# Layer 0's convolutions: the values' 1x1 products ahead of the first depthwise product, and VectorE's taps dealt anew

## The chip, the cores and the metric

The kernel runs on one core of a Trainium2 chip. The metric is the device time of one execution in microseconds, as the median of several runs. The kernel has 82,178 instructions on five engines that run side by side, each through its own list in order: TensorE (PE, with its weight loads as PEld), VectorE (DVE), ScalarE (ACT), GpSimd (POOL) and SyncE (SP), which issues DMAs.[...]

## The reference

Four layers are applied one after the other to `x` of shape 2 x 128 x 64 x 64, each as `x = x + layer(groupnorm(x))`. Only layer 0 is touched:

```python
xn = biasfree_ln(x, ln1_w)
qkv = conv1x1(xn, w_qkv)                      # 128 -> 5 * 128 channels
qkv = conv_general_dilated(qkv, w_dw, 3x3, 'SAME', feature_group_count=5 * c)
q1, k1, v, q2, k2 = jnp.split(qkv, 5, axis=1)
q1, q2, k1, k2 = map(l2norm_tokens, (q1, q2, k1, k2))
attn1 = softmax(q1 . k1 * temperature)        # over the 4096 positions, 4 heads of 32 channels
attn2 = softmax(q2^T . k2 * temperature)      # over channels
out = attn1 . v  +  v . attn2
out = conv1x1(biasfree_ln(conv1x1(out, w_po), ln2_w), w_proj) + b_proj
```

So five groups of 128 channels (q1, k1, v, q2, k2) each go through a 1x1 product over channels, and then through nine taps of a 3x3 convolution with weights of their own for each channel.

## The kernel before, in words

Channels lie on the 128 partitions, the 4096 positions (64 rows of 64) along the free dimension. A sample's feature map is handled in two halves of 32 rows. For sample 0 and then for sample 1 the function `_layer0` runs `convolutions`, then `attention` (the softmax over positions, by far the longest part), then `finish` (the output products, layer norm and the addition to x). The finish of sample 0 is held back and runs inside the convolutions of sample 1.

`pointwise(pad, grp, half)` makes one *frame*: the 1x1 products of one group and one half, written into a padded image of 34 rows by 66 columns. GpSimd zeroes the borders (three memsets, L1582 to L1585), TensorE makes the products (L1591, ten instructions) and ScalarE copies them from PSUM into the frame in four pieces (L1598).

The 3x3 convolution of a half is done in one of two ways. `depthwise` does it on TensorE: 144 small matmuls with diagonal weights (L1613; the trace shows 288 instructions, since each float32 product is two), accumulating into two pairs of PSUM banks. `taps` does it on VectorE: a multiplication for the first tap (L1648) and eight multiply-adds (L1650), each over 128 x 2048 elements. It is a generator, and each `next` issues one tap. Three of the ten halves go to VectorE: the first half of k1 and both halves of the values v, 27 taps a sample. The other seven go to TensorE in the order `[(1,1), (0,0), (0,1), (3,0), (4,0), (3,1), (4,1)]` of (group, half); I number these stages n = 0 to 6.

PSUM is used in three pairs of banks (`sp()`, in turn) and two single banks (`acc(0)`, `acc(1)`). A depthwise product takes two pairs; a frame takes one pair and both single banks, `acc(0)` twice. After a depthwise product for q1 or k1 (n = 0, 1, 2), `in_place` copies the result out, eight 32 x 512 copies on ScalarE from the first pair and eight on VectorE from the second (L1633). After one for q2 or k2 (n = 3 to 6), ScalarE copies the first pair and VectorE the second (`copy`, L1624).

In stage n the program issues, in this order: the depthwise product; the copies out of it, and the frame for stage n + 2; ScalarE's sums of squares (L1638); what belongs to this stage alone; and then some of VectorE's taps. To this stage alone belong: a value frame and six steps of the earlier sample's finish at n = 0, the rest of the finish at n = 1, the other value frame and the norms of q1 and k1 (L1757 to L1760) at n = 2, the scaling of q1 (L1764) at n = 3, the token products of q2 and k2 (`products`, L1678 and L1688) at n = 4 and 6, and the transposes of the values (`value_tiles`, L1662) at n = 5 and 6. The order on each engine is that of the program (`_in_order`, L1328), so a copy waits behind the taps issued before it. How many taps each stage issues is the tuple at the end of the loop, one for sample 0 and one for sample 1.

Frames for TensorE lie in two buffers of the tag "pad", those for VectorE in two buffers of the tag "vpad"; each frame is 8,976 bytes a partition. The tile `qk2` (16,384 bytes) holds a half of q2 and k2 from n = 3 on.

Of the kernel before, what the change touches and what calls it, by code (L numbers as in the profile page):

```python
# [10 lines left out]
F32 = mybir.dt.float32  # L11
# [5 lines left out]
B, C, H, W = 2, 128, 64, 64  # L17
S = H * W
CH = 512
# [1429 lines left out]
def _layer0(ctx, tc, X, a, cst, worst, there, dram):  # L1449
# [8 lines left out]
    def sp():  # L1458
        n = at["pair"]
        at["pair"] = (n + 1) % 3  # L1460
        return banks[:, 2 * n : 2 * n + 2, :]

    def acc(n):
        return banks[:, 6 + n, :]
# [31 lines left out]
    v = one.tile([128, S], F32, name="v")  # L1496
# [3 lines left out]
    def inverse_norm(ss, name):  # L1500
        n = small.tile([128, 1], F32, tag=name, name=name)
        nc.vector.tensor_reduce(n, ss, AX.X, ALU.add)
        _power(nc, small, n, n, 1e-24, 0.0, mhalf)
        return n
# [72 lines left out]
    def frame(pool, tag="pad", bufs=2):  # L1577
        return pool.tile([128, H // 2 + 2, W + 2], F32, tag=tag, name=tag, bufs=bufs)

    def pointwise(pad, grp, half):  # L1580

        nc.gpsimd.memset(pad[:, :, 0:1], 0.0)  # L1582
        nc.gpsimd.memset(pad[:, :, W + 1 : W + 2], 0.0)
        edge = 0 if half == 0 else H // 2 + 1
        nc.gpsimd.memset(pad[:, edge, :], 0.0)  # L1585
        first, to = (0, 1) if half == 0 else (H // 2 - 1, 0)
        for r0, n in ((4 * ROWS, 1), (0, ROWS), (ROWS, 2 * ROWS), (3 * ROWS, ROWS)):
            ps = sp() if n > ROWS else acc(int(r0 == 0)).rearrange("p (o c) -> p o c", o=1)
            for i in range(0, n, ROWS):
                rows = min(ROWS, n - i)  # L1590
                nc.tensor.matmul(  # L1591
                    ps[:, i // ROWS, : rows * W],
                    w_qkv[:, grp * C : (grp + 1) * C],
                    xn[:, (first + r0 + i) * W : (first + r0 + i + rows) * W],
                    start=True,
                    stop=True,
                )
            nc.scalar.copy(  # L1598
                pad[:, to + r0 : to + r0 + n, 1 : W + 1],
                ps.rearrange("p k (h w) -> p (k h) w", w=W)[:, :n, :],  # L1600
            )
            yield

    def depthwise(grp, pad):


        ps = [sp() for _ in range(2)]
        for t in range(9):
            for c in range(4):
                for r in range(4):  # L1610
                    rows, to = slice(32 * r, 32 * r + 32), slice(32 * c, 32 * c + 32)
                    y0 = c * ROWS + t // 3
                    nc.tensor.matmul(  # L1613
                        ps[r // 2][to, r % 2, :].rearrange("p (h w) -> p h w", w=W),
                        diag[rows, grp, t, :],
                        pad[rows, y0 : y0 + ROWS, t % 3 : t % 3 + W],
                        start=(t == 0),
                        stop=(t == 8),
                    )
        return ps  # L1620

    def copy(out, in_):
        turn[0] += 1
        (nc.scalar.copy if turn[0] % 2 else nc.vector.tensor_copy)(out, in_)  # L1624

    def in_place(ps, half, out, p):


        for i in range(4):
            for n, engine in enumerate((nc.scalar.copy, nc.vector.tensor_copy)):  # L1630
                r, c = 2 * n + p, (i + 2 * n) % 4
                cols = slice((4 * half + c) * CH, (4 * half + c + 1) * CH)
                engine(out[32 * r : 32 * r + 32, cols], ps[n][32 * c : 32 * c + 32, p, :])  # L1633

    def squares(pool, t, at):
        junk = pool.tile([128, 2 * CH], F32, tag="junk", name="junk", bufs=1)
        n = t.free_size()
        nc.scalar.activation(junk[:, :n], t, AF.Square, accum_out=at)  # L1638

    def taps(grp, half, to, pad):  # L1640

        cols = slice(half * S // 2, (half + 1) * S // 2)
        out = to[:, cols].rearrange("p (h w) -> p h w", w=W)
        for t in range(9):
            x = pad[:, t // 3 : t // 3 + H // 2, t % 3 : t % 3 + W]
            tap = wd[:, 9 * grp + t : 9 * grp + t + 1]
            if t == 0:
                nc.vector.tensor_scalar_mul(out, x, tap)  # L1648
            else:
                nc.vector.scalar_tensor_tensor(out, x, tap, out, ALU.mult, ALU.add)  # L1650
            yield

    def squares_of(pool, out, half, at):
        for i in range(2 * half, 2 * half + 2):
            squares(pool, out[:, i * 2 * CH : (i + 1) * 2 * CH], at[:, i : i + 1])
# [41 lines left out]
    def convolutions(pool, b, before):  # L1697


        ss = small.tile([128, 2, 4], F32, tag="ss", name="ss")  # L1700
        ss2 = small.tile([128, 2, 4, 2], F32, tag="ss2", name="ss2")
        gram = None
        order = [(1, 1), (0, 0), (0, 1), (3, 0), (4, 0), (3, 1), (4, 1)]
        kpad = frame(pool, "vpad")
        run(pointwise(kpad, 1, 0))
        first = taps(1, 0, k1, kpad)
        frames = [frame(pool) for _ in range(2)]
        run(pointwise(frames[0], *order[0]))
        next(first)
        run(pointwise(frames[1], *order[1]))  # L1710
        by_vector = first

        def values_of(half):
            pad = frame(pool, "vpad")
            run(pointwise(pad, 2, half))
            return taps(2, half, v, pad)

        qk = None
        for n, (grp, half) in enumerate(order):
            ps = depthwise(grp, frames.pop(0))  # L1720
            following = iter(())
            if n + 2 < len(order):
                frames.append(frame(pool))
                following = pointwise(frames[-1], *order[n + 2])
            if grp >= 3:
                if grp == 3:
                    qk = pool.tile([128, 2, 4, CH], F32, tag="qk2", name="qk2", bufs=1)
                for p in range(2):
                    copy(qk[:, grp - 3, 2 * p : 2 * p + 2, :], ps[p])
                run(following)  # L1730
                for r in range(4):
                    squares(pool, qk[:, grp - 3, r, :], ss2[:, grp - 3, r, half : half + 1])
            else:
                out = (q1, k1)[grp]
                in_place(ps, half, out, 0)
                next(following, None)
                in_place(ps, half, out, 1)
                run(following)
                squares_of(pool, out, half, ss[:, grp, :])
            if n == 0:  # L1740
                by_vector = chain(by_vector, values_of(0))
                for _ in range(FIRST_PART):
                    next(before, None)
            elif n == 1:
                run(before)
            if n == 4:
                gram = acc(1)
                run(products(pool, qk, 0, gram))
            elif n == 5:
                run(value_tiles(0))  # L1750
            elif n == 6:
                run(value_tiles(1))
                run(products(pool, qk, 1, gram))
            if n == 2:
                squares_of(pool, k1, 0, ss[:, 1, :])
                by_vector = chain(by_vector, values_of(1))
                nq = inverse_norm(ss[:, 0, :], "nq1")  # L1757
                nk = inverse_norm(ss[:, 1, :], "nk1")
                sc = small.tile([128, 1], F32, tag="sc", name="sc")
                nc.vector.scalar_tensor_tensor(sc, nq, nk, temp, ALU.mult, ALU.mult)  # L1760
            if n == 3:
                for c in range(0, NCH, 2):
                    cols = slice(c * CH, (c + 2) * CH)
                    nc.vector.tensor_scalar_mul(q1[:, cols], q1[:, cols], sc)  # L1764
            for _ in range(((5, 5, 5, 4, 4, 4, 0), (2, 6, 6, 4, 4, 4, 0))[b > 0][n]):
                next(by_vector, None)

        own = small.tile([128, 4, C], F32, tag="own", name="own", bufs=1)
        nc.vector.tensor_mul(
            own,  # L1770
            gram.rearrange("p (r c) -> p r c", r=4),
            blocks.unsqueeze(1).to_broadcast([128, 4, C]),
        )
        return ss2, own
# [206 lines left out]
    def run(gen):  # L1981
        for _ in gen:
            pass

    def chain(*gens):
        for g in gens:
            yield from g
# [3 lines left out]
    with _in_order(tc):  # L1991
        first = normalize(0)
# [585 lines left out]
```

## Time and profile before

| | us |
|---|---|
| median of 3 runs | 4053.4 (4051.79 to 4055.28) |
| the profiled execution | 4055.8 |
| its span, first to last instruction | 4054.0 |
| normalizing sample 0 | 0 to 33.6 |
| convolutions of sample 0 | 33.6 to 193 |
| attention of sample 0 | 193 to 780 |
| convolutions of sample 1, with the finish of sample 0 | 780 to 975 |
| attention of sample 1 | 975 to 1568 |
| layers 1 to 3 | 1568 to 4054 |

A row of the profile in order of time reads: start, duration, engine, line, operation, output <- inputs, partitions x elements, how many such instructions in a row; and in brackets how long the engine had been idle before it and what ended that. A table of stretches has for each stretch its length, then the busy time of each engine with its number of instructions, then TensorE's granted clock as a share of full speed, the busy share of the DMA engines, and GB/s.

### The profile page before, as it was taken

The numbers are of one execution on the slowest core, as the hardware profiler recorded it, in microseconds if no ns is written. First come the engines' busy times: TensorE is split into PE (matmuls) and PEld (weight loads), VectorE is DVE, ScalarE is ACT, GpSimd is POOL, SyncE is SP. The second block draws the span as 40 slices with busy tenths as digits, with TensorE's granted clock in tenths as the row PEclk, the third lists the DMA queues.
The fourth block names the chain that finished last, engine by engine and source line by source line (L and its number), as shares of the span: only waits on it lengthen the run. The fifth ranks groups of instructions, "written<-read, shape, count | busy, mean of one in ns | idle before, by whom it ended". The sixth has DMA issues, their size and how long they took to land.

```text
span 4054.0 us, 82178 instructions
## 1 busy us (share of the span) xinstructions
PE 3872.8 (96%) x35214; PEld 1324.0 (33%) x35214; DVE 3198.9 (79%) x3572; ACT 3242.3 (80%) x3955; POOL 90.7 (2%) x145
## 2 busy tenths in 40 slices
PE   7899999989999998997998999999999999999998
PEld 4511221244121114445665222232222322222222
DVE  5699999766999998996766787777777777776666
ACT  4489889735899993325654899999999999999998
POOL 1000000010010001000000000000000000000000
PEclk9999999999999998998998999999999999999999
DMA  1199960000000000003663110110002000110000
GB/s 50 17 197 187 185 105 2 1 2 2 2 2 2 2 2 13 6 1 150 278 259 112 53 40 27 45 55 27 27 29 73 25 27 30 39 52 6 6 6 4
DMA packets 193128, 217.59 MB, mean 54 GB/s; under 512 B 30441, under 2 KB 154345, under 8 KB 188658
## 3 DMA queue, kind: packets, MB, share of 16 engines
q1 hardware_dynamic: 192754, 212.25, 20.3%
q8 instruction: 278, 4.55, 0.5%
q14 instruction: 96, 0.79, 0.1%
HBM read 178.64 MB, written 98.57 MB: 68 GB/s over the span
## 4 chain that ended last, share of the span: by engine, by line
PE 65%; DVE 7%; ACT 2%; issue 2%; POOL 0%; SPq 0%; DMA 0%; ACTq 0%; POOLq 0%; DVEq 0%
PE ps_acc L2293 25%; PE ps_s L2270 18%; PE ps L1842 5%; PE ps L1850 5%; PE ps_bank L710 2%; DVE sums L1873 2%; PE ps_z L1008 2%; DVE e L950 2%; PE ps_t L640 1%; PE ps_bank L590 1%; PE ps_bank L681 1%; PE ps_bank L1062 1%; PE ps_acc L2151 1%; PE ps_acc L2197 1%; PE ps_pe L925 1%
## 5 line engine op out<-in xcount | busy, mean ns | idle before, releaser
L2284 ACT ACTIVATE weights<-ps_s 128x1024 f32<-128x1024 f32 x1920 | 1781.4, 1062 | 75.6 <-PE ps_s L2270 75.5
L2293 PE MATMUL ps_acc<-weights,vt 128*32 128x512 f32 x8192 | 1092.7, 605 | 0.0
L1873 DVE TENSOR_TENSOR sums<-sums,weights 128x2048 f32<-128x2048 f32 x384 | 855.3, 2287 | 15.8 <-ACT weights L1921 14.5
L2270 PE MATMUL ps_s<-q,k 64*128 64x512 f32 x4096 | 831.0, 470 | 3.7 <-DMA k<-stack 2.5
L1921 ACT ACTIVATE weights<-ps 128x1536 f32<-128x1536 f32 x512 | 740.6, 1446 | 8.9 <-PE ps L1850 8.9
L2270 PEld LDWEIGHTS ps_s<-q,k 64*128 64x128 f32 x4096 | 348.4, 184 | 935.7 <-ACT weights L2284 809.2
L1850 PE MATMUL ps<-q,k 32*64 32x512 f32 x8192 | 577.0, 615 | 21.6 <-ACT weights L1918 19.4
L1842 PE MATMUL ps<-weights,vt 128*32 128x512 f32 x4096 | 548.3, 607 | 0.0
L2242 DVE SCALAR_TENSOR_TENSOR exp_z<-exp_z,exp_m 128x1024 f32<-128x1024 f32 x384 | 469.1, 1222 | 9.3
L1918 ACT ACTIVATE weights<-ps 128x512 f32<-128x512 f32 x512 | 306.8, 599 | 107.1 <-DVE sums L1873 38.6
L2226 DVE TENSOR_SCALAR exp_i<-ps_s 128x1024 int32<-128x1024 f32 x128 | 156.8, 1225 | 216.2 <-PE ps_s L2270 216.0
L1850 PEld LDWEIGHTS ps<-q,k 32*64 32x64 f32 x8192 | 120.8, 130 | 456.4 <-ACT weights L1918 403.4
L2293 PEld LDWEIGHTS ps_acc<-weights,vt 128*32 128x32 f32 x8192 | 161.9, 108 | 309.3 <-issue 308.5
L1842 PEld LDWEIGHTS ps<-weights,vt 128*32 128x32 f32 x4096 | 84.4, 108 | 392.7 <-issue 379.4
L662 DVE SCALAR_TENSOR_TENSOR X<-g,w,X 128x2048 f32<-128x2048 f32 x84 | 197.4, 2351 | 2.6
L1873 DVE TENSOR_TENSOR sums<-weights 128x2048 f32<-128x2048 f32 x64 | 145.9, 2289 | 39.8 <-ACT weights L1921 39.3
L2246 DVE SCALAR_TENSOR_TENSOR weights<-exp_z,exp_i 128x1024 f32<-128x1024 f32 x128 | 156.8, 1225 | 15.9 <-ACT weights L2284 0.5
L2242 DVE SCALAR_TENSOR_TENSOR exp_z<-exp_m 128x1024 f32<-128x1024 f32 x128 | 156.0, 1219 | 0.0
L1008 PE MATMUL ps_z<-w_ri,e 128*32 128x128 f32 x2048 | 137.3, 408 | 14.1 <-DVE e L950 11.9
L1613 PE MATMUL ps<-pad,diag 32*32 32x512 f32 x4032 | 142.3, 604 | 4.1 <-ACT vt L1624 3.7
L1591 PE MATMUL ps<-xn,w_qkv 128*128 128x512 f32 (+1 forms) x200 | 87.3, 583 | 22.5 <-ACT pad L1598 14.1
L950 DVE TENSOR_SCALAR e<-ps_pe 32x136 f32<-32x136 f32 (+1 forms) x352 | 104.3, 296 | 4.9
(304 smaller groups left out, 2976.7 us busy)
## 6 DMA issues: line engine op xcount, KB each, us to landing
w_ri<-w_r SPq DMA_DIRECT2D x16, 2112.0 KB, 8.0
w_ri<-w_i SPq DMA_DIRECT2D x16, 2112.0 KB, 13.6
stack<-qs SPq DMA_DIRECT2D x64, 256.0 KB, 2.1
q<-stack SPq DMA_DIRECT2D x128, 128.0 KB, 2.5
k<-stack SPq DMA_DIRECT2D x128, 128.0 KB, 2.6
stack<-ks SPq DMA_DIRECT2D x32, 256.0 KB, 2.2
w_r<-in_L_conv_kr_w SPq DMA_DIRECT2D x15, 528.0 KB, 12.6
w_r<-in_L_conv_kr_x SPq DMA_DIRECT2D x15, 528.0 KB, 12.6
```

Source lines behind the costliest of these rows:

```text
L662: nc.vector.scalar_tensor_tensor(xi, g[:, i : i + H // 2, j : j + W], w8[:, s : s + 1], xi, ALU.mult, ALU.add)
L950: nc.vector.tensor_scalar_mul(out, got[of, :, s], sign)
L1008: nc.tensor.matmul(out.rearrange("p (n f o) -> p n f o", n=2, f=2), e[:, s, 2 * j : 2 * j + 2, :].rearrange("p f x -> p (f x)"), w.rearran ...
L1842: nc.tensor.matmul(out[rows, :], lhs(rows), w[:, j, :], start=first, stop=stop)
L1850: nc.tensor.matmul(bank[64 * h : 64 * h + 64, :], k1[rows, kt * 128 + 64 * h : kt * 128 + 64 * h + 64], q1[rows, qb * CH : (qb + 1) * CH], ...
L1873: nc.vector.tensor_add(parts[p].rearrange("p j c -> p (j c)"), t.rearrange("p j c -> p (j c)"), w.rearrange("p j c -> p (j c)"),)
L1918: nc.scalar.activation(held[n][:, 0, :], single, AF.Exp)
L1921: nc.scalar.activation(held[n][:, 1:, :], three, AF.Exp)
L2242: nc.vector.scalar_tensor_tensor(z, x, n, m, ALU.add, ALU.mult)
L2270: nc.tensor.matmul(ps[j // 2][:, j % 2, :], g.k[kt // 4][rows, j // 2, keys], g.q[qb][rows, j // 2, :], start=True, stop=True,)
L2284: nc.scalar.activation(w[0], ps[p], AF.Exp)
L2293: nc.tensor.matmul(g.ac[32 * j : 32 * j + 32, :], g.vt[:, kt, j // 2, i : i + 2, :].rearrange("p a d -> p (a d)"), w[:, i, :], start=(at = ...
```

## The change

The first half of k1 gets its frame from the tag `qk2`, which is free until stage 3, so that both buffers of "vpad" can hold the two value frames at once. All five first frames are then made before the loop: k1's, those of stages 0 and 1, and the two value frames. Behind each of the last four, VectorE is given two taps of k1, so eight of the nine are issued before the first depthwise product. The value frames disappear from stages 0 and 2. Nineteen taps are left for the loop, dealt in new numbers: 3, 3, 3, 2, 4, 4 in sample 0 (before 5, 5, 5, 4, 4, 4, of which the last call is empty) and 0, 2, 4, 4, 4, 5 in sample 1 (before 2, 6, 6, 4, 4, 4).

```diff
         order = [(1, 1), (0, 0), (0, 1), (3, 0), (4, 0), (3, 1), (4, 1)]
-        kpad = frame(pool, "vpad")
+        kpad = pool.tile([128, 8 * CH], F32, tag="qk2", name="kpad", bufs=1)
+        kpad = kpad[:, : (H // 2 + 2) * (W + 2)].rearrange("p (h w) -> p h w", w=W + 2)
         run(pointwise(kpad, 1, 0))
         first = taps(1, 0, k1, kpad)
         frames = [frame(pool) for _ in range(2)]
-        run(pointwise(frames[0], *order[0]))
-        next(first)
-        run(pointwise(frames[1], *order[1]))
-        by_vector = first
+        by_vector = [first]
+
+        def ahead():
+            for _ in range(2):
+                next(first)
 
         def values_of(half):
             pad = frame(pool, "vpad")
             run(pointwise(pad, 2, half))
-            return taps(2, half, v, pad)
+            by_vector.append(taps(2, half, v, pad))
+
+        for n in range(2):
+            run(pointwise(frames[n], *order[n]))
+            ahead()
+        for n in range(2):
+            values_of(n)
+            ahead()
+        by_vector = chain(*by_vector)
...
             if n == 0:
-                by_vector = chain(by_vector, values_of(0))
                 for _ in range(FIRST_PART):
                     next(before, None)
...
             if n == 2:
                 squares_of(pool, k1, 0, ss[:, 1, :])
-                by_vector = chain(by_vector, values_of(1))
                 nq = inverse_norm(ss[:, 0, :], "nq1")
...
-            for _ in range(((5, 5, 5, 4, 4, 4, 0), (2, 6, 6, 4, 4, 4, 0))[b > 0][n]):
+            for _ in range(((3, 3, 3, 2, 4, 4, 0), (0, 2, 4, 4, 4, 5, 0))[b > 0][n]):
                 next(by_vector, None)
```

## The prediction

> **What bounds the kernel now.** I read the busy shares first, then the stretches of the kernel, and then the instructions in order of time in the only two stretches that the diff touches: the convolutions of sample 0 (33.6 to 193 us) and of sample 1 (780 to 975 us). First the page's shares, then the stretch table (busy us of PE, PEld, DVE, ACT, POOL; clock; DMA):
>
> ```profile
> PE 3872.8 (96%) x35214; PEld 1324.0 (33%) x35214; DVE 3198.9 (79%) x3572; ACT 3242.3 (80%) x3955; POOL 90.7 (2%) x145
> ...
> 33.60:193.00 159.40, 144.50 (x2305) 84.64 (x2311) 95.46 (x83) 69.10 (x127) 6.30 (x25) 0.95 0.01 2
> 780.00:975.00 195.00, 165.68 (x2494) 101.08 (x2492) 117.62 (x167) 73.71 (x134) 12.79 (x40) 0.96 0.01 2
> ```
>
> DMA is idle there (0.01), and VectorE and ScalarE are 38 to 60% busy, so neither is the bound by sum. TensorE is busy 91% and 85%, so the stretch ends when its in-order list ends, and what counts are its waits. Sample 0 in order of time:
>
> ```profile
> 48.65 3.92 PE L1591 MATMUL ps<-xn,w_qkv 128*128 128x64 f32 x10 [0.73 <-ACT pad L1598]
> ...
> 62.37 5.62 DVE L1633 COPY k<-ps 32x512 f32<-32x512 f32 x8 [17.11 <-PE ps L1613]
> ...
> 69.28 6.55 PE L1591 MATMUL ps<-xn,w_qkv 128*128 128x64 f32 x9 [3.17 <-ACT pad L1598]
> ...
> 90.97 10.48 PE L1613 MATMUL ps<-pad,diag 32*32 32x512 f32 x286 [0.18 <-ACT q L1633]
> ...
> 114.22 9.75 PE L1613 MATMUL ps<-pad,diag 32*32 32x512 f32 x288
> ...
> 126.12 1.23 DVE L1624 COPY qk<-ps 128x1024 f32<-128x1024 f32 x1
> ...
> 127.76 9.77 PE L1613 MATMUL ps<-pad,diag 32*32 32x512 f32 x288
> ```
>
> A frame's 1x1 products take 3.92 us of TensorE, 4.65 from one frame to the next at the start (44.00, 48.65). VectorE idles 17.11 us there. The value frame's products inside the loop (69.28) are dearer: they wait 3.17 us for a copy queued on ScalarE and then run 6.55 instead of 3.92 us. Sample 1 has the same places, worse:
>
> ```profile
> 816.83 0.89 DVE L1511 BATCH_NORM_STATS2 ln_st<-ps 128x6 f32<-128x128 f32 x4 [7.04 <-PE ps L1962]
> ...
> 891.87 2.08 PE L1591 MATMUL ps<-xn,w_qkv 128*128 128x512 f32 x2 [6.08 <-ACT vpad L1598]
> ...
> 893.87 11.67 PE L1613 MATMUL ps<-pad,diag 32*32 32x512 f32 x288
> ...
> 906.15 1.23 DVE L1624 COPY qk<-ps 128x1024 f32<-128x1024 f32 x1
> ```
>
> **What the Trainium skill says.** "TensorE: Matmul & The Clock Gate", Architectural detail: ScalarE and VectorE are strict FIFO. The trace agrees: the copy of 126.12 starts when the last tap before it ends (126.09), 2.2 us after its depthwise product. The same page, What's actually happening: after an idle window of about 3.4 us the array runs at half clock until it has been busy about as long. The trace agrees in part: after 3.17 us idle the granted clock was 0.52 (69.2 to 75.8), 0.71 (108.4 to 114.2) or 1.00 (811 to 815). "VectorE: DVE Perf Modes", tier table: single-source fp32 runs at twice the rate of two-source. Here the first tap takes 1.28 us, the others 2.35 (2.38 from one to the next).
>
> **The change, part by part.** I call En the end of depthwise product n, read as the start of the TensorE group behind it: before, sample 0 has E0 62.19, E1 85.89, E2 101.38, E3 123.90, E4 137.46; sample 1 has 803.99, 843.64, 875.63, 905.47, 919.01.
>
> *Start.* Two more frames before depthwise 0: 2 x 4.65 = +9.3 us. Their ScalarE copies (2.3 us a frame) are inside that pace; no DMA moves, so SP has nothing of it. E0 becomes 71.5 and 813.3. Eight taps of the first keys, 1.3 + 7 x 2.38 = 18 us, run from 43.98 (785.85 in sample 1) to 62 (804): wholly in VectorE's idle time, cost nothing; without that cover each would cost up to 2.38. The memsets of two more frames (POOL, 0.16 us each) come early; the key frame's new place in qk2 has to be free only by depthwise 3, long after its ninth tap.
>
> *Sample 0, n=0.* Without the value products the stage is like n=1 before, which had none: E2-E1 = 15.49 us (1x1 products 3.9 us, then the wait until ScalarE and VectorE have emptied both PSUM pairs, 5.8 us after En, then 9.65 us). Before, E0 to E1 took 23.70: -8.2. VectorE: eight copies 5.62 and three taps (6.1) fit into 15.5. E1 = 87.0, E2 = 102.5, so +1.1 so far.
>
> *Sample 0, n=2.* The value products go here too. The norms keep their chain (ScalarE's squares, GpSimd's powers): the taps start at E2+12.82 (114.20). Three taps, 7.13: E2+19.95, but depthwise 3 now ends at E2+15.49. The VectorE copy of qk is behind those taps, 4.5 us late, done at E2+21.2. Depthwise 4 needs the PSUM pair it frees (its own products would let it start at E2+19.35). So 1.9 us of new wait, and E4 = E2 + 21.25 + 9.65 = E2+30.9 against 36.08 before: -5.2. Together E4 133.4 against 137.46: **-4.1 us**.
>
> *Sample 1, n=0.* Behind the pointwise products stands finish of sample 0. VectorE's first bn_stats waits until 816.83, 12.84 after E0, for products queued behind the value frame. Now TensorE reaches those at E0+3.8, VectorE is free at E0+5.8: start at 819.15, +2.3 instead of +9.3. The finish then has its own pace (3.8 us a chunk, VectorE, GpSimd, TensorE in turn) and E0 to E2 is otherwise unchanged: E2 = 877.9. Taps moved out of n=0 cost nothing (VectorE waited 1.45 us before E1); two instead of six at n=1 take away VectorE's 5.4 us delay at E2 (881.03 against 875.63).
>
> *Sample 1, n=2.* Four taps: E2+12.82+9.51 = E2+22.3, copy done E2+23.6, depthwise 4 ends at E2+33.3 = 911.2 against 919.01: **-7.8 us**. The new TensorE wait before depthwise 4 is 4.3 us, which can put the clock to half: depthwise 3 of before (893.87), after such waits, took 11.67 instead of 9.76, 1.9 more. Bounds 0 and 3; I take 1.3.
>
> *Behind it.* The copy after E4 comes 2.6 us late in sample 1 (four taps at n=3), done at E4+3.8; the product that needs its bank runs from E4+4.3: hidden. E4 to E5 is 26.04 in both samples and ends on ScalarE's squares and the token copies, which don't change. The fifth tap at n=5 in sample 1 ends 0.7 us after E6, so the second value transposes start late; ScalarE reads them only behind 4 us of squares: hidden, 0 to 0.7. The attention's first weights tile now lies on qk2: its exponential may wait 1 us, where the next one has 4.6 us of idle: hidden. Later stages only shift.
>
> Sum: -4.1 - 7.8 + 1.3 = **-10.6 us**. The profiled execution took 4055.8 (span 4054.0), 2.4 above the median of 4053.4; so 4045.2 for it, and **4042.8** as a median. The 18.6 us paid in front are the sure part; 8.2, 5.2, 7.0 and 10.1 less 1.3 have to be earned back in four stages.
>
> **Rivals.**
> (a) A part isn't earned. If the finish in sample 1 starts no earlier (its PSUM bank or GpSimd pacing it), 7 us are lost: 4049.8. For it: its VectorE-GpSimd chain has idle gaps everywhere. Against: the 7.04 us wait names TensorE. Within 0.2%.
> (b) VectorE's late copies don't hold depthwise 4, because the tail of the taps hides elsewhere; then all of E3 counts, -5.9 and -12.1: -18, 4035.4. Against: strict order on VectorE, and two PSUM pairs of three are taken by depthwise products.
> (c) Slower: the clock. Depthwise 1 to 4 of both samples now start after waits of 1 to 4 us without value products between. From about 2.5 us lost on each of the eight (20 us) the change is slower than before by 8; the row at 893.87 shows 1.9, and at 69.2 to 75.8 a whole group ran at 0.52. At 3 us each: 4053.4 - 11.9 + 24 = 4065.5. Against: depthwise 2 (90.97) followed such a wait at clock 1.00.
> (d) It doesn't do what it says: hardly, the order is fixed per engine by the program.
>
> **How the numbers follow.** Likeliest case 0.66 (4038 to 4047, of it 0.08 above 4045.3), (b) 0.08, (a) 0.13, (c) 0.11, (d) 0.02. A measurement of this kernel can tell 0.2%, 8.1 us, from no change: below 4045.3 is faster, above 4061.5 slower. Faster 0.66, same 0.08 + 0.13 + 0.02 = 0.23, slower 0.11. The range goes from 4036 to 4053: it takes in (a) and the clock's bound, and leaves out most of (b) and (c), under 0.2.
>
> **What would show it.** Right: four 1x1 groups of 4.65 us and eight key taps ahead of depthwise 0, E0 near 71.5 and 813; E0 to E1 15.5 us in sample 0; first bn_stats of the finish near 815 (819 less sample 0's gain); VectorE's qk copy behind n=2's taps, and TensorE waiting for it before depthwise 4, 2 and 4 us. E6 4 us earlier in sample 0, 10 to 12 in sample 1. Wrong: TensorE at half clock through whole depthwise products; a wait of the first frames for the attention's tiles in sample 1; attention stretches (587 and 593 us) of another length.

## The result, and the profile after

| | median, us | runs | ratio to before, 95% |
|---|---|---|---|
| before | 4052.6 (4046.74 to 4055.28) | 6 | |
| after | 4036.61 (4032.69 to 4038.05) | 6 | 0.9962 [0.9949, 0.9975] |
| after, once more | 4038.11 (4034.54 to 4042.41) | 6 | 0.9968 [0.9956, 0.998] |

The change makes the kernel faster, by 16 us in the first comparison and by 12.7 in the second (there against 4050.82, the median of 37 runs of before). Forecast were 4042.8 for the median, with a range of 4036 to 4053, and 10.6 us for the gain; so the first median lies 0.6 us above the range's lower end. The profiled execution of after took 4035.3 us, its span is 4033.5.

The page of after, busy shares of the engines:

```profile
PE 3863.0 (96%) x35214; PEld 1317.6 (33%) x35214; DVE 3198.8 (79%) x3572; ACT 3242.7 (80%) x3955; POOL 90.5 (2%) x145
```

Every count is the same as before (35,214, 3572, 3955, 145): the change only moves work. So the gain must lie in the waiting or in TensorE's clock. To see it, both kernels have to be cut at the same events. I cut each convolution stretch from the first tap on the first half of k1 (L1648) to VectorE's product that makes `own` (L1769 before, L1777 after), the last of `convolutions`. Before, in the table of stretches (length, then busy PE, PEld, DVE, ACT, POOL; clock; DMA):

```profile
43.98:192.65 148.67, 135.26 (x2280) 79.62 (x2288) 91.93 (x71) 64.25 (x119) 3.65 (x23) 0.94 0.01 2
785.85:972.55 186.70, 158.72 (x2456) 98.90 (x2464) 113.17 (x159) 69.63 (x127) 11.77 (x31) 0.95 0.01 2
```

After, the same cuts:

```profile
39.44:183.93 144.49, 134.71 (x2280) 78.85 (x2288) 92.02 (x70) 64.65 (x119) 3.01 (x17) 0.98 0.01 2
773.69:954.03 180.34, 159.71 (x2456) 99.25 (x2464) 113.08 (x159) 70.02 (x127) 11.06 (x25) 0.97 0.01 2
```

The two stretches together shrink from 335.37 to 324.83 us, by 10.5. TensorE's busy time in them is 293.98 before and 294.42 after, so its idle time fell from 41.4 to 30.4. (The split is rough: the same work counts as longer busy where the clock is low, and the clock column is lower before; and rows such as the one at 72.04 below, 10.48 us for 286 instructions where 288 take 9.76 elsewhere, hold some waiting.) VectorE has 205.1 us of work in both. The forecast's 10.6 us are in these two stretches; what the first comparison shows beyond them is dealt with below.

Sample 0 of after in order of time, the lines that answer to those shown of before:

```profile
40.76 16.68 DVE L1650 SCALAR_TENSOR_TENSOR k<-kpad,wd,k 128x2048 f32<-128x2048 f32 x7
...
53.43 3.92 PE L1591 MATMUL ps<-xn,w_qkv 128*128 128x64 f32 x10 [0.73 <-ACT vpad L1598]
57.29 9.76 PE L1613 MATMUL ps<-pad,diag 32*32 32x512 f32 x288
...
67.15 5.62 DVE L1633 COPY k<-ps 32x512 f32<-32x512 f32 x8 [9.71 <-PE ps L1613]
...
72.04 10.48 PE L1613 MATMUL ps<-pad,diag 32*32 32x512 f32 x286 [0.17 <-ACT k L1633]
...
110.68 7.12 DVE L1650 SCALAR_TENSOR_TENSOR v<-vpad,wd,v 128x2048 f32<-128x2048 f32 x3
...
117.83 1.22 DVE L1624 COPY qk<-ps 128x1024 f32<-128x1024 f32 x1
119.11 9.72 PE L1613 MATMUL ps<-pad,diag 32*32 32x512 f32 x284 [0.92 <-DVE qk L1624]
```

The keys' taps (40.76) now run while TensorE makes the four frames; VectorE still idles 9.71 us before its first copy, where it idled 17.11. Depthwise 1 (72.04) follows depthwise 0 with only the normal wait for PSUM: the value products with their 3.17 us wait and their 6.55 us are gone from this place. The last two lines are the new wait: the copy of qk stands behind three taps, and depthwise 4 cannot go on until that copy has emptied its PSUM pair. (Four of its 288 instructions, 1.05 us, run before the row's wait of 0.92 us; counted from the end of the 1x1 products the delay is 1.9 us.)

In sample 1 of before, the copies behind stage 1 came late, because five taps stood before them (E2 was at 875.63):

```profile
869.10 11.90 DVE L1650 SCALAR_TENSOR_TENSOR k<-vpad,wd,k 128x2048 f32<-128x2048 f32 x5
881.03 5.62 DVE L1633 COPY q<-ps 32x512 f32<-32x512 f32 x8
```

Sample 1 of after in order of time:

```profile
806.97 0.89 DVE L1511 BATCH_NORM_STATS2 ln_st<-ps 128x6 f32<-128x128 f32 x4
...
866.14 5.62 DVE L1633 COPY q<-ps 32x512 f32<-32x512 f32 x8 [5.56 <-PE ps L1613]
...
878.77 9.51 DVE L1650 SCALAR_TENSOR_TENSOR v<-vpad,wd,v 128x2048 f32<-128x2048 f32 x4
...
888.31 1.22 DVE L1624 COPY qk<-ps 128x1024 f32<-128x1024 f32 x1
...
889.59 10.99 PE L1613 MATMUL ps<-pad,diag 32*32 32x512 f32 x284 [3.23 <-DVE qk L1624]
```

The finish's first bn_stats starts without a wait, 5.8 us after E0 (801.15); before it waited 7.04 us for TensorE and came 12.84 us after E0. The copies at 866.14 now wait for TensorE; before they came 5.4 us after TensorE was done. The last lines are the new wait in its larger form: four taps, the copy of qk, then TensorE released after 3.23 us (4.2 us after the end of the 1x1 products) and running 10.99 us for 284 instructions (9.72 in sample 0).

**Where the profiled difference of 20.5 us lies.** The stages of the two first profiles, cut at the same events (us):

| | before | after | difference |
|---|---|---|---|
| start to k1's first tap | 43.98 | 39.44 | -4.5 |
| convolutions of sample 0 | 148.67 | 144.49 | -4.2 |
| attention of sample 0 | 593.20 | 589.76 | -3.4 |
| convolutions of sample 1 | 186.70 | 180.34 | -6.4 |
| attention of sample 1 | 565.68 | 565.40 | -0.3 |
| its finish | 46.66 | 45.53 | -1.1 |
| layer 1 | 258.11 | 256.03 | -2.1 |
| layers 2 and 3 | 2211.0 | 2212.5 | +1.5 |

Attention ends here at its last copy of q, the finish of sample 1 at the first product of layer 1 (L590 in before), layer 1 at the first `ps_py` product of layer 2 (L883). Half of the difference lies in stages that the diff does not touch. Whether that is a consequence or chance was the first question.

### The profile page after: what moved, and what is told of

The parts are those of the page before. It is cut to its first block, busy times and chain, and to the rows that moved or that the text cites. A ratio compares the mean times of both kernels' runs of the same rounds, so it can differ in the third digit from the quotient of the medians.

```text
span 4033.5 us, 82173 instructions
## 1 busy us (share of the span) xinstructions
PE 3863.0 (96%) x35214; PEld 1317.6 (33%) x35214; DVE 3198.8 (79%) x3572; ACT 3242.7 (80%) x3955; POOL 90.5 (2%) x145
## 3 DMA queue, kind: packets, MB, share of 16 engines
q8 instruction: 278, 4.55, 0.5%
## 4 chain that ended last, share of the span: by engine, by line
PE 77%; DVE 10%; ACT 4%; issue 4%; POOL 0%; SPq 0%; DMA 0%; ACTq 0%; DVEq 0%; POOLq 0%
PE ps_acc L2301 25%; PE ps_s L2278 19%; PE ps L1850 9%; PE ps L1858 9%; DVE sums L1881 5%; PE ps_z L1008 2%; PE ps_bank L710 2%; PE ps L1613 1%; PE ps_t L640 1%; ACT weights L1929 1%; DVE e L950 1%; PE ps_bank L590 1%; PE ps_bank L1062 1%; PE ps_bank L681 1%; ACT weights L1926 1%
## 5 line engine op out<-in xcount | busy, mean ns | idle before, releaser
L1881 DVE TENSOR_TENSOR sums<-sums,weights 128x2048 f32<-128x2048 f32 x384 | 855.1, 2285 | 12.9 <-ACT weights L1929 11.9
L1858 PE MATMUL ps<-q,k 32*64 32x512 f32 x8192 | 575.9, 614 | 21.2 <-ACT weights L1926 18.9
L1613 PEld LDWEIGHTS ps<-pad,diag 32*32 32x32 f32 x4032 | 84.4, 103 | 68.1 <-issue 19.1
```

Of the source, the lines that this page charges most:

```text
L1613: nc.tensor.matmul(ps[r // 2][to, r % 2, :].rearrange("p (h w) -> p h w", w=W), diag[rows, grp, t, :], pad[rows, y0 : y0 + ROWS, t % 3 : t ...
L1858: nc.tensor.matmul(bank[64 * h : 64 * h + 64, :], k1[rows, kt * 128 + 64 * h : kt * 128 + 64 * h + 64], q1[rows, qb * CH : (qb + 1) * CH], ...
L1881: nc.vector.tensor_add(parts[p].rearrange("p j c -> p (j c)"), t.rearrange("p j c -> p (j c)"), w.rearrange("p j c -> p (j c)"),)
```

## The experiments

Medians are of the runs of each kernel; ratios are to the kernel before on the same chip. "Stretches" is the sum of the two convolution stretches in the run's profile, with the cuts above.

### Both kernels again

Both kernels unchanged.

> The changed kernel once more. Theory 1 (the two convolution stretches alone earn 4.2 and 6.4 us; the rest of the first comparison was TensorE's clock, which is at half or full speed by chance while sample 0 is normalized and at the start of its attention): the gain is nearer 10.6 us than 16, and in the new profile the distance from k1's first finished frame to the end of depthwise product 4 is 89.4 us again in sample 0 while the time up to that frame may be 39.4 or 44.0. Theory 2 (the change also speeds up what lies outside the two stretches): 15 to 16 us again, with the first frame at 39.4 us and the attention of sample 0 3.4 us shorter than before.

> The kernel before once more, for the chance in it. Theory 1: within 0.1% of itself, the runs split into two groups about 5 us apart, and the new profile may have its first frame at 39.4 instead of 44.0 us with the stretch from there to the end of depthwise product 4 unchanged at 93.5. Theory 2: the first frame at 44.0 us again, attention of sample 0 587 us again.

The kernel after gave 4038.11 and the ratio in the table above; its first frame was done at 43.2 us and E4 of sample 0 came 89.3 us later, as theory 1 expected. The kernel before gave 4050.22 (13 runs), ratio 0.9998 [0.9989, 1.0006]: that is how finely the comparison tells two equal kernels apart. Here theory 1 missed twice: from the first frame to E4 of sample 0 it took 90.4 us and not 93.5, so that stretch has chance in it too, and the 13 times don't fall into two groups. Two more executions of the kernel before:

> The kernel before, one more look. Outside the two convolution stretches and the start, the two profiles of before so far spent 3.4 us more between the second attention's start and layer 2 (565.7, 46.7 and 258.1 us against 565.4, 45.5 and 256.0 with the change). Chance of the clock: one of the stages at the shorter time here. A consequence of the program: 565.7, 46.7 and 258.1 once more. The two stretches, from k1's first tap: 145 to 149 and 187 to 189 us either way.

> The same question as in the third look, on another execution.

They took 4047.24 and 4043.25 us (one execution each). The stages of all six profiles:

| us | start | conv. 0 | attention 0 | conv. 1 | finish of sample 1 | layer 1 | layers 2 and 3 |
|---|---|---|---|---|---|---|---|
| before | 43.98 | 148.67 | 593.20 | 186.70 | 46.66 | 258.11 | 2211.0 |
| before_again | 39.16 | 145.40 | 590.15 | 188.40 | 46.67 | 258.15 | 2213.2 |
| before_third | 41.75 | 147.16 | 590.07 | 188.64 | 46.73 | 255.81 | 2209.5 |
| before_fourth | 39.25 | 145.15 | 590.21 | 188.49 | 46.68 | 258.14 | 2207.8 |
| after | 39.44 | 144.49 | 589.76 | 180.34 | 45.53 | 256.03 | 2212.5 |
| after_again | 43.23 | 142.76 | 589.72 | 180.00 | 45.56 | 256.05 | 2212.8 |

The start is between 39 and 44 us long in either kernel: the 4.5 us of the first pair were chance. So were the 3.4 us of the attention: 593.20 never came again, and it is the one of the six with 10.2 us of recorded half clock in that stage instead of 3.4. Layer 1 was 255.81 in a run of before too. The finish of sample 1 was 1.1 us shorter in both profiles of after and in none of before, but it was 46.64 in a later kernel with the same order of frames (redeal_again below), so nothing is claimed of it. What separates the two kernels in every profile is the sum of the two convolution stretches: 335.4, 333.8, 335.8, 333.6 before (mean 334.65), 324.8 and 322.8 after (mean 323.8). **The gain of the change in these stretches is 10.9 us by the means** (8.8 to 13.0, depending on which pair of profiles is compared), against 10.6 forecast.

The forecast's sum ends at E4. Up to there the gain is 9.3 us by the means: from the first tap to E4, 91.9 to 89.3 in sample 0 (2.6) and 134.2 to 127.5 in sample 1 (6.7). The other 1.6 us lie behind E4, where chance shows: E4 to E5 takes 26.0 us in some executions of either kernel and 24.4 in others.

In sample 0 the kernel before has its own scatter, and one row of before_again in order of time shows it:

```profile
64.46 3.92 PE L1591 MATMUL ps<-xn,w_qkv 128*128 128x64 f32 x10 [3.16 <-ACT pad L1598]
```

The same products after the same wait as at 69.28 in the first profile (3.17 us), but all ten in 3.92 us, where nine of them took 6.55 there. E0 to E1 took 20.6 us here, 23.7 there. The record of the granted clock names the difference: it stood at half from 68.67 to 75.50 us in the first profile, and at full speed from 25.1 to 100.2 in this one. Over the four profiles of before E0 to E1 took 20.6 to 23.7 us, so the saving of 8.2 us at n = 0 that the forecast read from one profile is between 5.1 and 8.2. In sample 1 the first profile was the favourable one: E0 to E1 took 39.64 there and 41.3 to 41.4 in the three others, a saving of 7.0 or 8.7.

The start has the same cause. Its transposes in groups of four, in after_again and in before_again:

```profile
27.11 1.11 PE L1559 MATMUL ps<-consts,gn 128*128 128x128 f32 x4
```

```profile
27.07 0.66 PE L1559 MATMUL ps<-consts,gn 128*128 128x128 f32 x4 [0.15 <-ACT gn L1539]
```

One execution has the long start with 1.11 us a group, the other the short one with 0.66; here it is the kernel after that has the long one. The stretch table from 20 to 36 us, for after_again:

```profile
20.00:36.00 16.00, 13.81 (x50) 9.13 (x48) 12.59 (x67) 11.06 (x18) 9.05 (x8) 1.00 0.00 1
```

and before_again:

```profile
20.00:36.00 16.00, 11.59 (x57) 7.31 (x56) 13.65 (x70) 11.59 (x19) 10.12 (x8) 1.00 0.00 1
```

TensorE is busy 13.81 us for 50 instructions in the one and 11.59 us for 57 in the other. The clock column says 1.00 in both, but it measures nothing here in after_again: the trace's record of the granted clock has no entry before 40.7 us in after_again and before 25.1 in before_again, and the table prints a stretch without an entry as 1.00. In before_again the transposes change from 1.06 us a group (at 22.5 us) to 0.70 (25.0) and 0.66 just where the record begins. All eleven profiles without added work agree: the five whose record begins at 33 to 41 us have starts of 40.4 to 44.0 us, the six whose record begins at 24.5 to 25.5 have 39.0 to 39.8. So the start's length follows the moment at which TensorE's clock comes up, and that moment varies from execution to execution.

### The frames alone, the taps alone

The first takes from the change only the place of the frames: one tap ahead as before, and the old numbers.

```diff
         def ahead():
-            for _ in range(2):
+            for _ in range(1):
                 next(first)
...
             run(pointwise(frames[n], *order[n]))
-            ahead()
+            if n == 0:
+                ahead()
         for n in range(2):
             values_of(n)
-            ahead()
...
-            for _ in range(((3, 3, 3, 2, 4, 4, 0), (0, 2, 4, 4, 4, 5, 0))[b > 0][n]):
+            for _ in range(((5, 5, 5, 4, 4, 4, 0), (2, 6, 6, 4, 4, 4, 0))[b > 0][n]):
```

> Only the frames are moved: both value frames ahead of the loop and k1's frame in qk2, but one tap ahead and the old numbers of taps. Theory A (VectorE's list decides: the frames alone only move the wait from the products to the copies behind the taps): in sample 0 five taps and eight copies are 17.5 us in a stage of 15.5, E2 to E4 becomes 35.7, in all 3 us slower than before; in sample 1 the copies at n = 2 come 5.4 us late and six taps hold depthwise product 4, 1.5 us slower. Together 3 to 6 us slower than before, 14 to 17 slower than the change. Rival (the value products inside the loop were the cost): 8 to 10 us faster than before, close to the change.

The second takes only the taps; the value frames stay in stages 0 and 2, k1's frame in "vpad" (diff against the kernel before):

```diff
-        run(pointwise(frames[0], *order[0]))
-        next(first)
-        run(pointwise(frames[1], *order[1]))
+        for n in range(2):
+            run(pointwise(frames[n], *order[n]))
+            for _ in range(4):
+                next(first)
...
-            for _ in range(((5, 5, 5, 4, 4, 4, 0), (2, 6, 6, 4, 4, 4, 0))[b > 0][n]):
+            for _ in range(((3, 3, 3, 2, 4, 4, 0), (0, 2, 4, 4, 4, 5, 0))[b > 0][n]):
```

> Only the taps are dealt anew: eight taps of k1 ahead (four behind each of the two frames), the new numbers after that, the value frames left at n = 0 and n = 2. Theory A: sample 0 unchanged (0 us), since its stages end on TensorE there; in sample 1 VectorE is no longer 5.4 us late at E2, E2 to E3 falls from 29.8 to 22.5: 7.3 us faster than before, 3.3 slower than the change. Rival (the taps follow the frames and are worth nothing alone): the same as before within 2 us.

| us | median | ratio to before, 95% | against before | stretches |
|---|---|---|---|---|
| frames_only (19 runs) | 4057.3 | 1.0016 [1.0009, 1.0023] | +6.5 | 343.6 (+9.0) |
| taps_only (10 runs) | 4041.2 | 0.9977 [0.9967, 0.9986] | -9.6 | 327.7 (-6.9) |
| both: after_again | 4038.11 | 0.9968 [0.9956, 0.998] | -12.7 | 322.8 |

The frames alone make the kernel slower, so taking the value products out of n = 0 and n = 2 is no gain by itself, and the rival, in which it is the source of the gain (8 to 10 us), falls. Theory A's 3 to 6 us were too few. The reason shows in the profile of frames_only, sample 0 in order of time:

```profile
84.35 5.62 DVE L1633 COPY q<-ps 32x512 f32<-32x512 f32 x8
90.03 12.44 PE L1613 MATMUL ps<-pad,diag 32*32 32x512 f32 x282 [1.79 <-DVE q L1633]
...
115.19 11.89 DVE L1650 SCALAR_TENSOR_TENSOR v<-vpad,wd,v 128x2048 f32<-128x2048 f32 x5
127.12 1.22 DVE L1624 COPY qk<-ps 128x1024 f32<-128x1024 f32 x1
128.40 12.15 PE L1613 MATMUL ps<-pad,diag 32*32 32x512 f32 x284 [5.66 <-DVE qk L1624]
```

TensorE's stages have become shorter and VectorE's have not, so VectorE's copies are what TensorE waits for, at n = 1 (1.79 us, behind five taps and eight copies) and at n = 2 (5.66 us, behind five taps). After both waits the depthwise product runs at 12.44 and 12.15 us, 2.9 and 2.5 more than that many instructions take otherwise (9.76 us for 288). E1 to E2 was 20.3 us (17.5 expected) and E2 to E4 38.1 (35.7 expected): 2.8 and 2.4 us more, which is the slower product and not a longer wait. It happened twice more in sample 1 (14.59 us after a wait of 2.10, 11.81 after 3.85). The loss is not the clock's alone, though: up to E4 TensorE did 24.3 us of its work at a recorded half clock here and 17.7 on average before, which is worth 3.3 us at most, while the way from the first tap to E4 became 10.6 us longer in the two samples together.

The taps alone gain most of what the change gains, and 3.9 us less than it by the stretches (3.3 expected). In its profile of sample 1 VectorE is no longer late at E2 (868.79), and E2 to E3 took 22.5 us as expected, after 29.8 before (1.9 us of the difference is that depthwise 3 was slow there, 11.67 us instead of 9.76):

```profile
868.98 5.62 DVE L1633 COPY q<-ps 32x512 f32<-32x512 f32 x8 [5.56 <-PE ps L1613]
```

The two parts don't add up: +9.0 and -6.9 in the stretches, but -10.9 together. With the old numbers the moved frames cost 9.0 us; with the new ones they gain 3.9 (327.7 to 323.8). A shorter list on TensorE is worth something only where VectorE's list between two copies is short enough to follow.

### One size changed: the taps at n = 2

If the new wait before depthwise 4 is what the forecast said (the copy of qk behind n = 2's taps), then its length follows the time of those taps, 2.38 us for a multiply-add and 1.32 for a multiplication, from one to the next. Two kernels deal the same nineteen taps otherwise. Fewer at n = 2:

```diff
-            for _ in range(((3, 3, 3, 2, 4, 4, 0), (0, 2, 4, 4, 4, 5, 0))[b > 0][n]):
+            for _ in range(((4, 3, 2, 3, 4, 3, 0), (2, 3, 2, 4, 4, 4, 0))[b > 0][n]):
```

> The change with its nineteen taps dealt differently: 4, 3, 2, 3, 4, 3 in sample 0 and 2, 3, 2, 4, 4, 4 in sample 1, so two taps instead of three and four at n = 2. Theory A (VectorE's copy behind the taps of n = 2 holds depthwise product 4): the copy is done at E2+18.8, before TensorE wants it at E2+19.3; E2 to E4 becomes 29.0 in both samples, against 30.9 and 34.6 to 35: 7.4 us faster than the change, 18 to 21 faster than before. Rival (something else, the PSUM pairs or ScalarE's squares, holds it): within 2 us of the change.

and more:

```diff
-            for _ in range(((3, 3, 3, 2, 4, 4, 0), (0, 2, 4, 4, 4, 5, 0))[b > 0][n]):
+            for _ in range(((3, 1, 5, 2, 4, 4, 0), (0, 1, 5, 4, 4, 5, 0))[b > 0][n]):
```

> The change with more taps at n = 2: 3, 1, 5, 2, 4, 4 in sample 0 and 0, 1, 5, 4, 4, 5 in sample 1. Theory A: depthwise product 4 starts 2 x 2.38 us later in sample 0 and 2.38 later in sample 1: 7 us slower than the change, and up to 2 more if the longer wait puts TensorE's clock to half. Rival: within 2 us of the change, since the other taps move to places where VectorE waits anyway.

| us | taps at n = 2 | E2 to E4 | stretches | median | ratio to before, 95% |
|---|---|---|---|---|---|
| redeal | 2 and 2 | 28.98 and 29.04 | 315.9 | 4024.34 (5 runs) | 0.9943 [0.993, 0.9957] |
| after | 3 and 4 | 30.89 and 34.55 | 324.8 | 4036.61 (6 runs) | 0.9962 [0.9949, 0.9975] |
| after_again | 3 and 4 | 30.89 and 35.87 | 322.8 | 4038.11 (6 runs) | 0.9968 [0.9956, 0.998] |
| more_at_2 | 5 and 5 | 37.4 and 36.95 | 333.8 | 4044.24 (13 runs) | 0.9994 [0.9986, 1.0002] |

The profile of redeal, sample 1 in order of time:

```profile
875.56 4.73 DVE L1650 SCALAR_TENSOR_TENSOR v<-vpad,wd,v 128x2048 f32<-128x2048 f32 x2
880.32 1.23 DVE L1624 COPY qk<-ps 128x1024 f32<-128x1024 f32 x1
882.11 9.76 PE L1613 MATMUL ps<-pad,diag 32*32 32x512 f32 x288
```

With two taps the copy is done before depthwise 4 begins: no wait, 288 instructions in one row, 9.76 us. In more_at_2, sample 0:

```profile
123.60 1.23 DVE L1624 COPY qk<-ps 128x1024 f32<-128x1024 f32 x1
124.88 11.46 PE L1613 MATMUL ps<-pad,diag 32*32 32x512 f32 x284 [5.67 <-DVE qk L1624]
```

With five the wait is 5.67 us and the product is slow besides. The wait follows the taps exactly. In sample 0 two more multiply-adds (4.76 us) take it from 0.92 to 5.67. In sample 1 the fifth tap is a multiplication, since one tap fewer was issued before it, and the wait grows from 3.23 to 4.55, by 1.32 us; the 2.38 expected there were too many. So one dependence, taps at n = 2, copy of qk, PSUM pair, depthwise 4, sets this stage: of the 17.9 us between the stretches of redeal and more_at_2, 16.3 lie between E2 and E4, partly as waits and partly as slow products behind them. E0 to E2 is the same in all three kernels to 0.1 us, though their other numbers of taps differ there. By the medians the kernel moves from 4024 to 4044 us, and at 4044 nothing measurable is left of the change's gain: the interval holds 1, and the stretches are 333.8 where the kernel before has 334.65. The move of the frames and the eight taps ahead stayed the same in all three.

redeal beats both kernels. It was run once more:

> The new deal of the taps once more. If its gain over the change is the 7.2 us of the two stretches and the rest chance: 4026 to 4031 us. If it is the 13 us between the medians: 4022 to 4026 again. The two stretches 141 and 175 us either way.

4029.29 us (4027.52 to 4030.83, 4 runs) against 4051.97: ratio 0.9949 [0.9932, 0.9966], stretches 315.4 (140.8 and 174.6), as expected if the stretches are the gain. By the stretches redeal is 19 us faster than before, inside the expected 18 to 21, and 8.2 faster than the kernel after (315.6 against 323.8, 7.4 expected). By the medians it is 23 to 25 us less than before and, across different comparisons, 9 to 12 less than the kernel after.

### The clock at the start

To see whether TensorE's low activity causes the long start, idle TensorE was given products without use while sample 0 is normalized. Nothing reads them.

```diff
+        def busy(n):
+            for _ in range(n):
+                nc.tensor.matmul(acc(1), x[:, :128], x[:, :CH], start=True, stop=True)
+
+        if not within:
+            busy(4)
...
+                if not within:
+                    busy(1)
```

> The change with work added that nothing reads: 4 products of 128 x 512 on TensorE before the statistics of sample 0 and one behind each of its eight chunks. Theory 1 (while sample 0 is normalized, TensorE's clock is at half or full speed by chance, 4 to 5 us apart): with TensorE kept busy k1's first frame is done at 36.5 to 39.5 us in every execution, the median falls by 2 to 5 us below the change and the runs spread less. Theory 2 (the start differs for another reason, the loads of x): the first frame anywhere from 39 to 44 us, the median as with the change or up to 3 us slower for the added products.

The start took 37.81 us, less than in any other profile. The clock's record begins at 8.5 us, with full speed, where without the added products it began between 24.5 and 41.4. The transposes, in order of time, run at 0.66 us a group from early on:

```profile
17.85 0.66 PE L1566 MATMUL ps<-consts,gn 128*128 128x128 f32 x4 [0.53 <-ACT gn L1546]
```

The median was 4034.04 (6 runs), ratio 0.9965 [0.9953, 0.9977]. That is no different from the kernel after (0.9962 and 0.9968), and the times don't spread less (6.4 us from lowest to highest, 5.4 and 7.9 in the kernel after). So the profile bears out theory 1 on the start, while the medians can't show whether the kernel gains. With the better numbers of taps as well:

> Both of the foregoing together. Theories A and 1: the gains add, 9 to 12 us faster than the change, near 4027 us. If only one holds, that one's gain.

4033.45 us (5 runs), 0.9958 [0.9944, 0.9971]: not better than redeal (0.9943, 0.9949), a miss. In its profile the convolutions are right (317.35), and the start is 39.46: the clock's record begins at 9.5 us, falls to half from 12.9 to 19.7, and the transposes take 1.11 us until then. Layers 2 and 3 took 2219.8 us, 7 to 12 more than in the profiles of before and after. The record has 106.9 us of half clock there against 77 to 96 in those six; against redeal (86.5) it is 20.4 us more, which at half speed is the 10.2 us by which this stage is longer than there.

## Why the prediction was right, point by point

The first profiles, step by step as the forecast priced them (us):

| step | forecast | before | after | measured |
|---|---|---|---|---|
| sample 0, first tap to E0 | +9.3 | 18.21 | 27.53 | +9.3 |
| E0 to E1 | -8.2 | 23.70 | 15.48 | -8.2 |
| E1 to E2 | 0 | 15.49 | 15.42 | -0.1 |
| E2 to E4 | -5.2 | 36.08 | 30.89 | -5.2 |
| sample 1, first tap to E0 | +9.3 | 18.14 | 27.46 | +9.3 |
| E0 to E1 | -7.0 | 39.65 | 32.63 | -7.0 |
| E1 to E2 | 0 | 31.99 | 32.18 | +0.2 |
| E2 to E4, with the clock | -10.1 + 1.3 | 43.38 | 34.55 | -8.8 |

- **The 18.6 us in front** were paid as priced: the four frames follow each other at 4.65 us (44.12, 48.77, 53.43), and the eight keys' taps are hidden.
- **Stage 0 becomes a stage like n = 1**: 15.48 us for 15.49. The step was sound, but its saving was read from an execution in which the value products had run slowly (6.55 us); over four profiles of before its size is 5.1 to 8.2.
- **The new wait before depthwise 4** is where it was put and as long: copy done at E2 + 21.2 in sample 0, E4 at E2 + 30.9. The kernels with two and with five taps at n = 2 show it by its cause. In sample 1 the clock's term, bounded by 0 and 3 and taken as 1.3, measured 1.4: 10.99 us, against 9.76 x 284 / 288 = 9.6. That it came so close was luck. In after_again the same product, behind the same wait, lost 2.7:

```profile
891.59 12.32 PE L1613 MATMUL ps<-pad,diag 32*32 32x512 f32 x284 [3.23 <-DVE qk L1624]
```

The stretch table over this product, first in after, then in after_again, has the clock at 0.87 and 0.76:

```profile
889.59:900.58 10.99, 10.99 (x285) 6.56 (x285) 10.88 (x8) 1.45 (x4) 0.00 (x0) 0.87 0.01 3
891.59:903.91 12.32, 12.32 (x285) 7.36 (x285) 11.91 (x8) 1.45 (x5) 0.00 (x0) 0.76 0.01 3
```
- **The finish in sample 1** starts 5.8 us after E0, as said. Rival (a), that it starts no earlier, is out.
- **What was called hidden behind E4** stayed so: E4 to E5 is 26.0 in both samples of the first profile, as before (24.4 in the second), and the fifth tap at n = 5 lets the transposes of the values wait 0.66 us (0 to 0.7 forecast) where nothing needs them.
- **Rival (b)**, late copies that don't hold depthwise 4, is out: TensorE waits for them in after, more_at_2 and frames_only. The median alone would not have said so: 4036.61 is nearer to (b)'s 4035.4 than to 4042.8, and below the band of 4038 to 4047 that was called likeliest. It takes the rows in order of time to tell the two apart.
- **Rival (d)**, that the change doesn't do what it says, is out by the rows shown: the frames and the taps are where the diff puts them.
- **Rival (c)**, the clock on eight products, did not happen in this kernel: only depthwise 4 of sample 1 ran slow before E4, by 1.4 and 2.7 us. The mechanism is real, however: frames_only has it on four products, at 2.2 to 5.0 us each, around the 2.5 from which (c) would have decided. And in this kernel the clock worked the other way: from the first tap to E4 TensorE did 17.7 us of its work in both samples at a recorded half clock before (mean of four profiles) and 7.7 after (of two), which is worth up to 5 of the 9.3 us. How much of that was hidden behind other waits is not shown; the forecast took it in unnamed, by pricing stage 0 at its measured length.

The forecast of the median, 4042.8, was 6 us above the first result and 5 above the second. The mechanism's sum is not what missed: it gave 10.6, where the six profiles give 9.3 up to E4 and 10.9 over the stretches. That it fits the first pair to 0.1 us has luck in it. The sum was built on that very profile of before, where E0 to E1 was the longest of the four profiles in sample 0 and the shortest in sample 1; by the means sample 0 gains 2.6 us up to E4 (4.1 forecast) and sample 1 gains 6.7 (6.5). The sum was made against a single profiled execution with a long start and a long attention (43.98 and 593.20, where the same kernel also has 39 and 590), and no chance was allowed for either. Of the 16 us in the first comparison, about 11 are the change's and about 5 are not explained by it; with 11 alone the median would have been near 4041.7. The second comparison's interval, 8 to 18 us, holds 10.9. Whether the 2 us between 10.9 and 12.7 are anything is not settled.

One thing the forecast left out. It counted the gain by place (four stages that earn back 30.5 us less 1.3), and this was right as a sum, but it said nothing of which part of the change earns it. The two halves show that the new numbers of taps earn most of it, 6.9 us without the frames, that the frames alone lose 9.0, and that they add 3.9 once the taps are dealt anew.

## What to carry to other kernels

When work is taken out of one engine's list, look at once at what the next engine has queued ahead of the copy that frees a buffer: a deferrable multiply-add before such a copy costs its whole length on the bound engine once the slack is used up, 2.4 us each here, and more where the wait brings the clock down. Deal the deferrable work by the slack between two such copies, not evenly; in this kernel that was worth another 8 us without any other edit. And for gains below half a per cent, cut several profiles at the same events: the stretches repeated to about 2 us where whole executions of one kernel scatter over 13 in one comparison (4045.5 to 4058.78).

## What the runs showed of the hardware that was not expected

- A granted clock of 1.00 in a table can mean that nothing was recorded. In all thirteen profiles the clock's record begins with a piece at full speed, 8.5 to 41.4 us after the start, and in the eleven without added products the groups of four transposes take 1.06 to 1.12 us ahead of that point (the first group more) and 0.65 to 0.70 behind it.
- The recorded clock was only ever 1.0 or 0.5, in pieces that are 3.41 us long or whole multiples of it (3.41, 6.83, 10.24 and so on, all but the last of an execution), and their edges lie at other moments in each execution. So the same wait can meet a half-clock piece in one execution and miss it in the next, as the two rows of depthwise 4 above show.
- So a slow depthwise product doesn't follow from the length of the wait before it. After 5.66 us it took 12.15 us, after 5.67 it took 11.46, after 3.23 it took 10.99 or 12.32, but after only 1.79 it took 12.44. It follows from how much of a half-clock piece falls on the product: in frames_only such a piece lay from 89.32 to 96.15 us and the product began at 90.03, so 6.1 us of it ran at half speed and should cost 3.1 us; 2.9 were measured. The Trainium skill ("TensorE: Matmul & The Clock Gate", What's actually happening) lets the clock fall after an idle window of about 3.4 us. The length of the pieces agrees with that; but the window need not be idle throughout. Counted over the thirteen traces in the recorded pieces of 3.41 us, the clock fell after every one of the 173 pieces at full speed in which TensorE was busy for less than 0.42 of the time, after none in which it was busy for more than 0.78, and after some of those between. What decides there was not tried.
